# The table of comparisons between a token's logits, moved from SBUF into the free part of the gates' PSUM bank

## The chip, the cores and the metric

The kernel runs on one core of a Trainium2 chip. The metric is the device time of one execution in microseconds (us); the figure given for a kernel is the median of its runs. All data are 32-bit floats.

## The reference

A decoder block over 16 sequences of 256 tokens, 512 wide: a state-space layer, a gated long convolution against a context, and a feed-forward layer with a base product and eight low-rank experts. The experts are where the change lies. Each token takes the two experts with the largest logits:

```python
def _L0_ffn_ref(x, W, b, lora_A, lora_B, gate_w, gate_b):
    K = 2
    ...
    base = x_flat @ W.T + b
    logits = x_flat @ gate_w.T + gate_b
    topk_logits, topk_idx = jax.lax.top_k(logits, K)
    gates = jax.nn.softmax(topk_logits, axis=-1)
    xA = jnp.einsum('nd,erd->ner', x_flat, lora_A)
    delta_all = jnp.einsum('ner,eor->neo', xA, lora_B)
    delta_topk = jnp.take_along_axis(delta_all, topk_idx[:, :, None], axis=1)
    lora_update = jnp.sum(delta_topk * gates[:, :, None], axis=1)
    out = base + SCALING * lora_update
...
x = _layernorm(x + _L0_attn_ref(x, ...), axis=-1)
x = _layernorm(x + _L0_xattn_ref(x, L0_xattn_k, fside_S2_0, ctx_2048, ctx_2048, 8), axis=-1)
x = _layernorm(x + _L0_ffn_ref(x, ...), axis=-1)
```

## The kernel before

The first stage (up to about 760 us) computes the state-space layer for eight groups of 512 tokens and stores the normalised result in `first`. The second stage does the convolution and the feed-forward layer. It is a loop over 32 heads `h` (`HX`), each of 8 positions of all 16 sequences, so 128 tokens. One pass of the loop works on several heads at once: the convolution of head `h`, the feed-forward of head `h - 1`, the low-rank product and the last normalisation of head `h - 2`, and the preparation of head `h + 1`. The order of the instructions on each engine is written out by hand (`manual_schedule`): an engine runs its own instructions in the order of the program, and semaphores connect the engines.

The convolution of a head has two halves, `q` = 0 and 1. In each half TensorE fills four PSUM banks, `y[0]` (blocks 1 and 0) and `y[1]` (blocks 2 and 3):

- `seeded` (L1012) multiplies the pair sums `xs` into the bank of block 3, in `y[1]`; ScalarE copies that to the bank of block 2 (L1019).
- `convolve` adds the full blocks (L1030) and the 64x64 quadrants of the diagonal (L1045).
- `multiplied` (L1080, VectorE) multiplies a pair of banks by the context, `y[1]` first; `reduced` (L1090) sums over eight neighbours. The pool `ps_y` has one buffer of each bank, so the next half's seed follows L1080's reading of `y[1]`.

VectorE also makes the products for the next head (`products`, L157: 128x1024, from a transposed tile in PSUM and the context in SBUF), the reduction `ws` (L942) and the start of the last normalisation (`x3`, L1151, in `finish`). POOL (GpSimd) makes `xs` (L996), differences of Toeplitz blocks `Td` (L1001), the skip products `sk` (L932), the output with residual `ol` (L1259), the folds of its squares (L1185) and the small powers.

The feed-forward of a head: `products_with_gates` puts the logits, the low-rank products `xA`, the mean and the mean square of 128 tokens into one PSUM tile `gl` (pool `ps_t`, two buffers of one bank, tag "tr"): columns 0 to 7 are the logits, 8 to 135 `xA` (`NG` = 136), 136 the mean, 137 the mean square. ScalarE squares the mean (`m2`, L1201), VectorE makes the variance (L1207), POOL the reciprocal root `rs`. Then `gates` turns logits into scaled low-rank products:

- L1118 and L1120: the logits `lg` and their negated maximum; L1122 on ScalarE the exponentials `ex`.
- L1127, L1128: for each of the 64 pairs of experts whether the other logit is equal, and whether it is greater, into the table `cmp` (8 x 2 x 8 words a token). L1129 keeps the equal ones of lower index, with the constant `tri`. L1131 sums the table to a rank.
- L1133: exponentials of the ranks under 1.5, with their sum `den`; L1136 its reciprocal; L1138 the scaled products `xa`, which read `gl` a last time.

In the next pass TensorE transposes `xa` (L1216) and adds the low-rank product (L1222). In the loop this comes just after the base products L1226 and just ahead of the seed L1012 of half 0; on VectorE, L1138 stands directly ahead of the two L1080 of half 1. The last head has no pass to follow: its end is written out after the loop, with `gl` in pool `ps_b` (L1341) and a call of `gates` at L1402. So `gates` is called 32 times.

Of the kernel before, what the change touches and what calls it, by code (L numbers as in the profile page):

```python
# [8 lines left out]
F32 = mybir.dt.float32  # L9
AF = mybir.ActivationFunctionType  # L10
ALU = mybir.AluOpType
# [3 lines left out]
P = 128  # L15
# [9 lines left out]
LN_EPS = 1e-05  # L25
# [6 lines left out]
NE, R = 8, 16  # L32
# [22 lines left out]
NG = NE + ER  # L55
# [3 lines left out]
def layer_norm_stats(nc, pool, nhalf, src, tag):  # L59

    st = pool.tile([P, 6], F32, tag=f"st_{tag}", name=f"st_{tag}")
    nc.vector.bn_stats(st, src)
    mv = pool.tile([P, 2], F32, tag=f"mv_{tag}", name=f"mv_{tag}")
    nc.vector.bn_aggr(mv, st)
    ve = pool.tile([P, 1], F32, tag=f"ve_{tag}", name=f"ve_{tag}")
    nc.vector.tensor_scalar_add(ve, mv[:, 1:2], LN_EPS)  # L66
    rs = pool.tile([P, 1], F32, tag=f"rs_{tag}", name=f"rs_{tag}")
    nc.gpsimd.tensor_tensor(rs, ve, nhalf[:, 0:1], ALU.pow)  # L68
    return mv, rs
# [3 lines left out]
def decoder_kernel(  # L73
# [43 lines left out]
    ps_t = ctx.enter_context(tc.tile_pool(name="ps_t", bufs=2, space=PSUM))  # L117
# [51 lines left out]
    def wait_for(ins, other):  # L169
        tc.add_manual_dep(  # L170
            ins.ins,
            other.ins.name,
            mybir.DependencyInfo(
                mybir.DependencyClass.Sync, mybir.DependencyReason.DATA
            ),
            reason="order",
        )
# [4 lines left out]
    with ExitStack() as s1:  # L182
# [3 lines left out]
        p2 = s1.enter_context(tc.tile_pool(name="p2", bufs=2))  # L186
# [366 lines left out]
        for g in range(groups):  # L553
# [97 lines left out]
            for i, (kind, p) in enumerate(order):  # L651
# [18 lines left out]
                if i == 9:  # L670
# [3 lines left out]
                    for ht in range(HT):  # L674
                        for b in range(GB):
# [4 lines left out]
                                start=(ht == 0),  # L680
                                stop=(ht == HT - 1),
# [67 lines left out]
            def gated(cc, pss):  # L749
# [10 lines left out]
            own = {  # L760
                (r, h): [zs[HC * h + c][:, r * S : (r + 1) * S] for c in range(HC)]
                for r in range(2)
                for h in range(2)
            }
# [99 lines left out]
            else:  # L864
                finish_sums()
                gated(1, spread_heads(1))
                for n, t in enumerate((0, 2, 1, 3)):
# [3 lines left out]
                    for c in range(NI):  # L871
                        for j in range(2):
# [4 lines left out]
                                start=(c == 0 and j == 0),  # L877
                                stop=(c == NI - 1),
                                skip_group_check=True,
# [13 lines left out]
            if g == 0:  # L893
                skip_bc = wp.tile([P, S], F32, name="skip_bc")
                nc.sync.dma_start(skip_bc, skip.partition_broadcast(P))
                w_gl = wp.tile([P, KD, NG + 1], F32, name="w_gl")
# [13 lines left out]
                share = wp.tile([P, P], F32, name="share")  # L910
# [5 lines left out]
    with ExitStack() as s2:  # L916
        w2 = s2.enter_context(tc.tile_pool(name="w2", bufs=1, reuse_waits="tile"))
        p2 = s2.enter_context(tc.tile_pool(name="r2", bufs=2, reuse_waits="tile"))
        ps_b = s2.enter_context(
            tc.tile_pool(name="ps_b", bufs=1, space=PSUM, reuse_waits="tile")  # L920
        )
# [189 lines left out]
            nc.gpsimd.tensor_tensor(rs, var, nhalf[:, 0:1], ALU.pow)  # L1111
            return nm, rs

        def gates(gl, rs):


            lg = p2.tile([P, NE], F32, tag="lg", name="lg")
            nc.vector.scalar_tensor_tensor(lg, gl[:, 0:NE], rs, gb_bc, ALU.mult, ALU.add)  # L1118
            nm = p2.tile([P, 1], F32, tag="nm", name="nm")
            nc.vector.tensor_reduce(nm, lg, AX.X, ALU.max, negate=True)  # L1120
            ex = p2.tile([P, NE], F32, tag="ex", name="ex")
            nc.scalar.activation(ex, lg, AF.Exp, bias=nm)  # L1122
            sq = [P, NE, NE]
            own = lg.unsqueeze(2).to_broadcast(sq)
            other = lg.unsqueeze(1).to_broadcast(sq)
            cmp = p2.tile([P, NE, 2, NE], F32, tag="cmp", name="cmp")
            nc.vector.tensor_tensor(cmp[:, :, 1, :], other, own, ALU.is_equal)  # L1127
            nc.vector.tensor_tensor(cmp[:, :, 0, :], other, own, ALU.is_gt)  # L1128
            nc.vector.tensor_tensor(cmp[:, :, 1, :], cmp[:, :, 1, :], tri, ALU.mult)  # L1129
            rank = p2.tile([P, NE], F32, tag="rank", name="rank")  # L1130
            nc.vector.tensor_reduce(rank, cmp, AX.XY, ALU.add)  # L1131
            den = p2.tile([P, 1], F32, tag="den", name="den")
            nc.vector.scalar_tensor_tensor(  # L1133
                ex, rank, 1.5, ex, ALU.is_lt, ALU.mult, accum_out=den
            )
            nc.vector.reciprocal(den, den)  # L1136
            xa = p2.tile([P, NE, R], F32, tag="xa", name="xa")
            nc.vector.scalar_tensor_tensor(  # L1138
                xa,
                gl[:, NE:NG].rearrange("p (e r) -> p e r", r=R),  # L1140
                den,
                ex.unsqueeze(2).to_broadcast([P, NE, R]),
                ALU.mult,
                ALU.mult,
            )
            return xa
# [12 lines left out]
        def store(h, x3, nb, rs):  # L1159
            res = p2.tile([P, D], F32, tag="res", name="res")  # L1160
            nc.scalar.activation(res, x3, AF.Identity, bias=nb, scale=rs)
            nc.sync.dma_start(out[h * P : (h + 1) * P, :], res)
# [15 lines left out]
        def squares(o_l):  # L1178

            sq = p2.tile([P, D], F32, tag="sq", name="sq")  # L1180
            nc.scalar.activation(sq, o_l.rearrange("p k t -> p (k t)"), AF.Square)

            def folded():
                for n in (D // 2, D // 4):
                    nc.gpsimd.tensor_tensor(sq[:, 0:n], sq[:, 0:n], sq[:, n : 2 * n], ALU.add)  # L1185

            return sq[:, 0:P], folded

        def products_with_gates(o_l, sq):

            gl = ps_t.tile([P, NG + 2], F32, tag="tr", name="gl")
            for kc in range(KD):
                nc.tensor.matmul(  # L1193
                    gl[:, 0 : NG + 1], o_l[:, kc, :], w_gl[:, kc, :],
                    start=(kc == 0), stop=(kc == KD - 1),
                )
            last = nc.tensor.matmul(
                gl[:, NG + 1 :], sq, share[:, 0:1], start=True, stop=True, skip_group_check=True
            )
            m2 = p2.tile([P, 1], F32, tag="m2", name="m2")  # L1200
            wait_for(nc.scalar.activation(m2, gl[:, NG : NG + 1], AF.Square), last)  # L1201
            return gl, m2

        def spread_of(gl, m2):

            var = p2.tile([P, 1], F32, tag="var_b", name="var_b")
            nc.vector.scalar_tensor_tensor(  # L1207
                var, gl[:, NG + 1 :], LN_EPS, m2, ALU.add, ALU.subtract
            )
            rs = p2.tile([P, 1], F32, tag="rs_b", name="rs_b")  # L1210
            nc.gpsimd.tensor_tensor(rs, var, nhalf[:, 0:1], ALU.pow)
            return rs

        def turned_gates(xa, at=None):
            xat = (at or ps_t).tile([ER, P], F32, tag="vp" if at else "tr", name="xat")
            nc.tensor.transpose(xat, xa.rearrange("p e r -> p (e r)"), ident)  # L1216
            xaT = p2.tile([ER, P], F32, tag="xaT", name="xaT")
            nc.scalar.copy(xaT, xat)
            return xaT
# [11 lines left out]
        for h in range(HX):  # L1231
# [8 lines left out]
            if h:  # L1240
# [6 lines left out]
                if rest is not None:  # L1247
                    base, o_r, xa = rest
# [6 lines left out]
            if ff:  # L1255
# [9 lines left out]
                sq, folded = squares(o_l)  # L1265
# [36 lines left out]
            if ff:  # L1302
                gl, m2 = products_with_gates(o_l, sq)
                rs = spread_of(gl, m2)
                base = ps_b.tile([P, D], F32, tag="base", name="base")
                feed_forward(base, o_l, (0,), True)
# [13 lines left out]
                sk_next = skip_sums(h + 1, kv_n)  # L1320
                more_next[2](1)
            if ff:
                xa = gates(gl, rs)
            if nxt:
                convolve(y, kv, T, Td, 1)
                rest = (base, o_l, xa) if ff else None
# [11 lines left out]

        o_f, red_f, y_f, cT_f = last
        tr = ps_t.tile([P, KD, P], F32, tag="tr", name="tr")  # L1340
        gl = ps_b.tile([P, NG], F32, tag="vp", name="gl")  # L1341
        o_l = {}

        def contracted(src, ks):
# [28 lines left out]
        def own(k):  # L1373
            return o_l[k].rearrange("p q t -> p (q t)")

        def norms_and_gates(*ks):
            for k in ks:
                nc.tensor.transpose(tr[:, k, :], own(k), ident)
            for k in ks:
                nc.tensor.matmul(  # L1380
                    gl, own(k), w_gl[:, k, 0:NG], start=(k == 0), stop=(k == 3),
                    skip_group_check=True,
                )

# [9 lines left out]
        contracted(y_f[2].unsqueeze(1), (2,))  # L1394
        contracted(y_f[1][:, 1:2, :], (3,))
        norms_and_gates(0, 1)
        feed(0)
        norms_and_gates(2, 3)
        for k in (1, 2, 3):
            feed(k)  # L1400
        _, rs = layer_norm_stats(nc, p2, nhalf, tr.rearrange("p c l -> p (c l)"), "b")
        xaT = turned_gates(gates(gl, rs))  # L1402
        store(*ready)
        nc.tensor.matmul(base, xaT, w_lb, start=False, stop=True, skip_group_check=True)
        x3 = p2.tile([P, D], F32, tag="x3", name="x3")
        nc.vector.scalar_tensor_tensor(x3, base, rs, b_bc, ALU.mult, ALU.add)
        mv, rs = layer_norm_stats(nc, p2, nhalf, x3, "c")
# [78 lines left out]
```

## Time and profile before

| | |
|---|---|
| median of 3 runs | 1428.67 us (1428.57 to 1429.22) |
| the profiled execution | 1429.05 us, of which the profile's span is 1427.3 |
| mean granted TensorE clock | 0.998 |
| busy over the span: TensorE, VectorE, ScalarE, POOL | 99%, 85%, 29%, 34% |
| busy from 790 to 1390 us: TensorE, VectorE, ScalarE, POOL | 599.7, 553.4, 173.6, 347.4 of 600 us |

The profile is one execution. Each instruction has a start, a duration and, where its engine sat idle before it, the event that ended the idle time. "PE" is a matmul and "PEld" the load of its stationary operand, which may overlap the matmul before it. A tensor operation in this kernel's convolution appears as two PE instructions. The ends of matmuls are modelled, so a busy TensorE isn't TensorE at its full rate. "Issue" is time in which an engine waited for nothing that the profile shows. The busy time of a VectorE instruction includes the time for which it is held up after it has started. Line numbers are those of the kernel before.

### The profile page before, as it was taken

The numbers are of one execution on the slowest core, as the hardware profiler recorded it, in microseconds if no ns is written. First come the engines' busy times: TensorE is split into PE (matmuls) and PEld (weight loads), VectorE is DVE, ScalarE is ACT, GpSimd is POOL, SyncE is SP. The second block draws the span as 40 slices with busy tenths as digits, with TensorE's granted clock in tenths as the row PEclk, the third lists the DMA queues.
The fourth block names the chain that finished last, engine by engine and source line by source line (L and its number), as shares of the span: only waits on it lengthen the run. The fifth ranks groups of instructions, "written<-read, shape, count | busy, mean of one in ns | idle before, by whom it ended". The sixth has DMA issues, their size and how long they took to land.

```text
span 1427.3 us, 18820 instructions
## 1 busy us (share of the span) xinstructions
PE 1413.3 (99%) x6882; PEld 906.7 (64%) x6882; DVE 1211.9 (85%) x2133; ACT 415.2 (29%) x902; POOL 492.4 (34%) x662
## 2 busy tenths in 40 slices
PE   8999999999999999999999999999999999999997
PEld 7788888887888888888884444444444444444443
DVE  6988878788888787887848999999999999999996
ACT  2423323233232332322302222222222232223221
POOL 5450011110100101002005556556555655565562
PEclk9999999999999999999999999999999999999999
DMA  8014111120211201212012221221122122212200
GB/s 300 33 39 131 45 47 45 38 83 8 69 60 38 83 9 39 82 45 84 15 38 85 67 63 55 72 70 57 62 67 74 45 74 67 65 54 74 67 26 23
DMA packets 49164, 89.15 MB, mean 62 GB/s; under 512 B 8880, under 2 KB 13360, under 8 KB 49072
## 3 DMA queue, kind: packets, MB, share of 16 engines
q1 hardware_dynamic: 49072, 87.96, 19.3%
q8 instruction: 54, 0.88, 0.3%
q14 instruction: 38, 0.31, 0.1%
HBM read 70.62 MB, written 17.32 MB: 62 GB/s over the span
## 4 chain that ended last, share of the span: by engine, by line
PE 97%; DVE 1%; issue 1%; DMA 0%; SPq 0%; POOL 0%; POOLq 0%; ACT 0%; DVEq 0%
PE mm L330 21%; PE y L1030 15%; PE s L330 14%; PE y L1045 12%; PE base L1226 8%; PE s L782 6%; PE mm L782 6%; PE y L1012 4%; PE gl L1193 2%; PE base L1222 2%; PE tr L147 1%; PE xm L599 1%; PE mm L739 1%; PE mm L873 1%; PE s L873 1%
## 5 line engine op out<-in xcount | busy, mean ns | idle before, releaser
L1080 DVE TENSOR_TENSOR pr<-y,cT 128x1024 f32<-128x1024 f32 x126 | 148.1, 1217 | 45.4 <-PE y L1045 45.4
L1045 PE MATMUL y<-kv 64*64 64x512 f32 x1536 | 179.6, 598 | 0.0
L588 DVE SCALAR_TENSOR_TENSOR acc<-xi,wc,acc 128x512 f32<-128x512 f32 x192 | 142.3, 755 | 7.4 <-ACT acc L584 1.7
L1090 DVE TENSOR_REDUCE red<-pr 128x128 f32<-128x1024 f32 x126 | 147.1, 1208 | 0.0
L157 DVE TENSOR_TENSOR kv<-tr,cT 128x1024 f32<-128x1024 f32 x124 | 145.4, 1213 | 0.0
L1030 PE MATMUL y<-kv 128*128 128x512 f32 x272 | 128.0, 594 | 1.8 <-DVE pr L1080 1.7
L1045 PEld LDWEIGHTS y<-kv 64*64 64x64 f32 x1536 | 52.2, 132 | 119.0 <-issue 96.7
L1226 PE MATMUL base<-w_f,ol 128*128 128x512 f32 x248 | 124.0, 603 | 0.0
L1030 PE MATMUL y<-kv,Td 128*128 128x512 f32 x248 | 116.5, 592 | 0.0
L68 POOL TENSOR_TENSOR rs_a<-ve_a,nhalf 128x1 f32<-128x1 f32 x32 | 19.0, 594 | 243.0 <-DVE ve_a L66 243.0
L1259 POOL TENSOR_TENSOR ol<-o,red 128x512 f32<-128x512 f32 x31 | 39.4, 1270 | 179.9 <-DVE red L1090 179.9
L391 POOL TENSOR_TENSOR rstd<-ms,nhalf 128x4 f32<-128x4 f32 (+1 forms) x9 | 8.5, 950 | 251.0 <-DVE ms L389 251.0
L1030 PEld LDWEIGHTS y<-kv 128*128 128x128 f32 x272 | 50.9, 189 | 67.8 <-issue 34.1
L330 PE MATMUL mm<-XT,w_z 128*128 128x256 f32 x384 | 90.7, 379 | 0.0
L1030 PEld LDWEIGHTS y<-kv,Td 128*128 128x128 f32 x248 | 47.1, 190 | 59.3 <-issue 59.3
L1019 ACT COPY y<-y 64x512 f32<-64x512 f32 x120 | 67.0, 558 | 56.3 <-PE y L1012 54.3
L996 POOL TENSOR_TENSOR xs<-kv 128x512 f32<-128x512 f32 x63 | 80.4, 1277 | 0.1
L330 PEld LDWEIGHTS mm<-XT,w_z 128*128 128x128 f32 x384 | 73.0, 190 | 9.9
L330 PE MATMUL mm<-xnT,w_z 128*128 128x256 f32 x288 | 70.8, 382 | 0.0
L1012 PE MATMUL y<-xs,kv 128*128 128x512 f32 x120 | 63.5, 611 | 0.7 <-issue 0.7
L1226 PEld LDWEIGHTS base<-w_f,ol 128*128 128x128 f32 x248 | 42.4, 191 | 30.9 <-issue 30.9
L330 PE MATMUL s<-XT,w_xi 128*128 128x256 f32 x256 | 61.0, 380 | 0.5 <-DVE XT L226 0.3
(283 smaller groups left out, 2814.7 us busy)
## 6 DMA issues: line engine op xcount, KB each, us to landing
cT<-in_ctxT SPq DMA_DIRECT2D x32, 384.0 KB
kv<-in_toep SPq DMA_DIRECT2D x32, 384.0 KB
xt<-in_x SPq DMA_DIRECT2D x32, 256.0 KB
spread<-both SPq DMA_DIRECT2D x32, 256.0 KB
first<-xt SPq DMA_DIRECT2D x32, 256.0 KB
vn<-first SPq DMA_DIRECT2D x32, 256.0 KB
out<-res SPq DMA_DIRECT2D x31, 256.0 KB
xnT<-in_xT SPq DMA_DIRECT2D x7, 1024.0 KB
```

The costliest lines, as they stand in the source:

```text
L157: last = nc.vector.tensor_tensor(kv[:, q, k * BQ : (k + NL // 2) * BQ], vT[:, q, blks].rearrange("p k (b i) -> p (k b) i", i=NH).unsqueeze ...
L330: nc.tensor.matmul(ps, w[:, p, a, kc, :], Xs[b][:, kc, :], start=start and kc == 0, stop=stop and kc == 1, skip_group_check=upon,)
L588: ins = nc.vector.scalar_tensor_tensor(acc, xi[:, :, k : k + S], wc[:, c, k : k + 1], acc, ALU.mult, ALU.add)
L782: nc.tensor.matmul(ps, own[a][c][:, n * P : (n + 1) * P], w_o[b][c], start=start and c == 0, stop=stop and c == HC - 1, skip_group_check=upon,
L996: return nc.gpsimd.tensor_tensor(xs[:, q], moving(kv, q, 0), moving(kv, q, 1), ALU.add)
L1012: nc.tensor.matmul(seed, T[:, SHARED_AT, :], xs[:, q], start=True, stop=True)
L1019: nc.scalar.copy(bank_of(y, 2)[b : b + HP], seed[a : a + HP])
L1030: nc.tensor.matmul(bank_of(y, lb), w, moving(kv, q, mb), start=not late and lb not in begun, stop=False, skip_group_check=True,)
L1045: return nc.tensor.matmul(bank_of(y, lb)[cols], T[rows, DIAGONAL_AT, (b - a) * HP : (b - a + 1) * HP], moving(kv, q, lb)[rows], start=star ...
L1080: nc.vector.tensor_tensor(pr.rearrange("p (k b j) i -> p k b j i", k=2, j=NH), y[i].rearrange("p k (b j i) -> p k b j i", j=NH, i=NH), cT[ ...
L1090: nc.vector.tensor_reduce(red[:, q, 2 * i : 2 * i + 2, :].rearrange("p k t -> p (k t)"), pr, AX.X, ALU.add)
L1226: nc.tensor.matmul(base, o_l[:, kc, :], w_f[:, kc, :], start=(first and kc == kcs[0]), stop=False)
```

## The change

The tile `cmp` in SBUF goes. Both tiles `gl` become wider by 2 x 8 x 8 = 128 words, and `gates` is handed these words and lays its table out in them. The bank's other columns keep their places; the matmul and the reading of the mean square name their one column instead of all from there on, and the last head's matmul names columns 0 to 135. Every instruction, its engine and its place in the order stay.

```diff
-        def gates(gl, rs):
+        def gates(gl, rs, room):
...
-            cmp = p2.tile([P, NE, 2, NE], F32, tag="cmp", name="cmp")
+            cmp = room.rearrange("p (a two b) -> p a two b", two=2, b=NE)
             nc.vector.tensor_tensor(cmp[:, :, 1, :], other, own, ALU.is_equal)
             nc.vector.tensor_tensor(cmp[:, :, 0, :], other, own, ALU.is_gt)
             nc.vector.tensor_tensor(cmp[:, :, 1, :], cmp[:, :, 1, :], tri, ALU.mult)
...
-            gl = ps_t.tile([P, NG + 2], F32, tag="tr", name="gl")
+            gl = ps_t.tile([P, NG + 2 + 2 * NE * NE], F32, tag="tr", name="gl")
...
-                gl[:, NG + 1 :], sq, share[:, 0:1], start=True, stop=True, skip_group_check=True
+                gl[:, NG + 1 : NG + 2], sq, share[:, 0:1],
+                start=True, stop=True, skip_group_check=True,
...
-                var, gl[:, NG + 1 :], LN_EPS, m2, ALU.add, ALU.subtract
+                var, gl[:, NG + 1 : NG + 2], LN_EPS, m2, ALU.add, ALU.subtract
...
-                xa = gates(gl, rs)
+                xa = gates(gl, rs, gl[:, NG + 2 :])
...
-        gl = ps_b.tile([P, NG], F32, tag="vp", name="gl")
+        gl = ps_b.tile([P, NG + 2 * NE * NE], F32, tag="vp", name="gl")
...
-                    gl, own(k), w_gl[:, k, 0:NG], start=(k == 0), stop=(k == 3),
+                    gl[:, 0:NG], own(k), w_gl[:, k, 0:NG], start=(k == 0), stop=(k == 3),
...
-        xaT = turned_gates(gates(gl, rs))
+        xaT = turned_gates(gates(gl, rs, gl[:, NG:]))
```

## The prediction

> **What bounds the kernel now.** I read the page first, then the chain that ended last in order of time, then the timeline around one call of `gates`. The page's fourth part says who sets the end:
>
> ```profile
> PE 97%; DVE 1%; issue 1%; DMA 0%; SPq 0%; POOL 0%; POOLq 0%; ACT 0%; DVEq 0%
> ```
>
> Taken alone this says that VectorE (DVE) work is free. Whether a matmul on that chain ran at its own pace has to be read from its pieces. The chain of one head in order of time (start, us, what):
>
> ```profile
> 1017.51 1.72 PE base L1226 x4
> 1019.23 0.11 PE xat L1216
> 1019.33 1.08 PE y L1012 x2
> 1020.41 0.86 PE base L1222 x2
> ...
> 1029.66 0.86 PE y L1012 x2
> ```
>
> Each tensor operation here is two instructions of 0.43 us. The seed matmul at line 1012 takes 0.86 us in one half of the head, but 1.08 where it follows the transpose of the gates (`xat`). So 0.22 us is lost in the second place. The transpose itself isn't the reason: near the end, at 1407.73, the same transpose is followed by four L1030 instructions in 1.72 us, which is 4 x 0.43 with nothing lost.
>
> The timeline shows what the seed waits for (DVE and POOL lines, then the weight load PEld; start, us):
>
> ```profile
> 1014.03 0.21 DVE L1127 TENSOR_TENSOR cmp<-lg 128x64 f32<-128x64 f32 x1
> 1014.10 1.49 POOL L932 TENSOR_TENSOR sk<-kv,skip_bc 128x512 f32<-128x512 f32 x1
> 1014.16 1.50 DVE L1128 TENSOR_TENSOR cmp<-lg 128x64 f32<-128x64 f32 x1
> 1015.53 1.28 POOL L996 TENSOR_TENSOR xs<-kv 128x512 f32<-128x512 f32 x1
> 1015.59 1.30 DVE L1129 TENSOR_TENSOR cmp<-cmp,tri 128x64 f32<-128x64 f32 x1
> ...
> 1017.33 0.17 DVE L1133 SCALAR_TENSOR_TENSOR ex<-rank,ex 128x8 f32<-128x8 f32 x1
> ...
> 1018.00 2.34 DVE L1080 TENSOR_TENSOR pr<-y,cT 128x1024 f32<-128x1024 f32 x2
> ...
> 1019.29 0.30 PEld L1012 LDWEIGHTS y<-xs,kv 128*128 128x128 f32 x2 [0.51 <-issue]
> ```
>
> The seed writes bank 3, in `y[1]`, which DVE reads with the first of the two L1080. That one ends at 1018.00 + 1.215 = 1019.21, and the weight load starts 0.08 later. The profile puts the pause down to "issue", but two other heads settle it: where L1080 starts at 1142.11 its end is 1143.32 and the load starts at 1143.39; from 1389.70 it is 1390.92 and 1390.99. The load follows it by 0.07 each time. In these two heads the chain shows 0.28 and 0.38 us of issue ahead of the seed as well. So TensorE is the engine of the chain, and DVE's queue holds it back once a head.
>
> On DVE two 128x64 operations cost 1.5 and 1.3 us. The trace's answers for single lines (ns min/median/max):
>
> ```profile
> L1127 DVE TENSOR_TENSOR cmp<-lg x32: 212/216/481, 787.0 to 1417.2; 128x64 f32<-128x64 f32 x32
> L1128 DVE TENSOR_TENSOR cmp<-lg x32: 215/1510/1527, 787.2 to 1417.4; 128x64 f32<-128x64 f32 x32
> L1129 DVE TENSOR_TENSOR cmp<-cmp,tri x32: 217/1303/1310, 788.6 to 1417.5; 128x64 f32<-128x64 f32 x32
> L1080 DVE TENSOR_TENSOR pr<-y,cT x126: 1211/1215/1226, 761.8 to 1400.3; 128x1024 f32<-128x1024 f32 x126
> L1151 DVE SCALAR_TENSOR_TENSOR x<-base,rs_b,b_bc x31: 737/740/748, 795.5 to 1410.6; 128x512 f32<-128x512 f32 x31
> ```
>
> Alone (the last two calls, with no POOL work beside them) all three take 0.21 to 0.22. In the other 30 heads L1128 ends as POOL's `sk` ends and L1129 as `xs` ends, 0.07 and 0.08 later. L1080 and L1151 have one input in PSUM and one in SBUF, run beside POOL's operations too (L1151 at 1022.52 beside `ol` from 1022.74), and never stretch.
>
> **What the Trainium skill says.** "SBUF — State Buffer", section "Who interferes with whom": a DVE instruction with two SBUF inputs contends with a GpSimd instruction that reads SBUF, whichever is second blocks until the other ends, and one with at most one SBUF input doesn't contend outside the two-port modes. The rows above agree: 1.3 to 1.5 us against a steady 1.215. "Perfetto Trace Analysis", section "Optimizing Scalar/DVE Operations": an access costs DVE about 60 ns in SBUF and 125 in PSUM. This trace shows no such difference for a PSUM input (L1080 1215 ns; L157 reads 1214 from PSUM and 1219 from SBUF); it has no DVE instruction that writes PSUM. "PSUM — Partial Sum Buffer", section "PSUM bank collisions raise a hardware error": two engines may not touch one bank's same partitions at once. Of this bank's other users the last, ACT's `m`, ends at 1028.90, and L1127 comes at 1034.66, so order costs nothing.
>
> **The change part by part.** It adds and removes no instruction, transfer or buffer: `gl` grows to 266 words, below the 512 of the other tiles of its tag. Four DVE instructions a call, 32 calls, change an operand's place.
>
> L1127 and L1128 still read `lg` twice from SBUF and write to PSUM. I keep them as they are: L1127 slips in between `Td` and `sk`, L1128 ends behind `sk` at 1015.66.
>
> L1129 now reads `cmp` from PSUM and `tri` from SBUF, the form of L1080. It should no longer wait for `xs`: 0.22 us instead of 1.30. In the call without POOL, L1133 starts 0.56 after the end of L1128 (1405.28 to 1405.84). Here that is 1015.66 + 0.56 = 1016.22 instead of 1017.33, or 1.11 earlier.
>
> **What is late next.** L1133 reads `rank` and `ex`, both in SBUF, and `xs` runs until 1016.81. By the same rule it blocks. Its form does so in this trace: an L588 at 22.89 beside POOL took 1.10 against a median of 0.75. It then ends at about 1016.89 as L1129 does now, against 1017.50: 0.61 earlier. I take 0.61; 1.11 is the other end.
>
> Price of PSUM as destination and for the reduction L1131: from 0 (the nearest rows, PSUM inputs) to 4 x 65 = 260 ns a call, my estimate from the skill's 125 - 60; a faster write than to SBUF can't be excluded, -50. I take 100 where nothing covers it. In the 30 heads the first 1016.81 - 1016.22 = 0.59 is covered by L1133's wait for `xs`; without that wait, 1.11 - 0.26 = 0.85 still remains.
>
> What the path gains: L1080 ends 0.61 earlier, at 1018.60, and the seed's load could start at 1018.67. TensorE wants it at the start of `xat`, 1019.06. It is ready 0.39 early and the pause goes. Over the 30 heads the pieces above 0.86 add up to 6.87 us, the issue ahead of them to 0.67: 7.54 in all. In the head at 1390 the pause is 0.24 + 0.38 = 0.62, just what DVE gives back; up to 0.05 may stay. The rest of DVE's 0.61 becomes idle time: before the other L1080 of a head it waits 1.35 us for L1045 now, and will wait about 1.35 + 0.61 - 0.23 = 1.7. `y[1]` can't be taken earlier than L1045 ends, 1016.92, which I have kept. POOL's `ol` and the folds start earlier, ahead of matmuls that don't wait for them.
>
> The last call (1417.2 to 1418.9) lies on the path with no POOL beside it: plus 0.1.
>
> Sum, against the profiled execution: 1429.05 - 7.54 + 0.05 + 0.1 = 1421.7. That execution is 0.38 above the median of 1428.67, so 1421.3 on the scale of the median.
>
> **The rivals.**
>
> *The gap is missed (slower).* L1127 starts 0.07 us ahead of `sk`. If, at its place between `Td` and `sk`, the PSUM destination makes it more than about 0.1 late, `sk` goes first: L1127 takes the 1.5 us, L1128 the 1.3, and L1129 comes after `xs` on top. L1131 then starts 0.16 behind L1128's end (as in the free call) where it now starts 0.04 behind L1129's, and two PSUM accesses add 0.13: 0.25 x 30 = 7.5 us, 1436. For it: the narrow margin. Against: at 1137.85 L1127 waited through `Td` (0.48 us) and still came ahead of `sk`. 6 in 100.
>
> *L1129 blocks all the same*, because the destination or `tri` takes the shared port. DVE loses 2 x 0.065 a head behind `xs`, 3.9 us, and 0.3 at the end, or nothing if PSUM is as cheap: 1428.7 to 1432.9. Against: L1080 and L1151. 4 in 100, half within 0.2%.
>
> *The pause is TensorE's own*, so that DVE only idles more: 1428.8. Against: the two heads where the load moved with L1080. 2 in 100.
>
> *Part of the gain*: L1128 or POOL shifts and 0.1 to 0.2 of each pause stays, 1423 to 1427. 6 in 100, most of it still over 0.2%.
>
> **How the numbers follow.** The main case has 82 in 100: 1420.3 (pause gone, a PSUM write slightly cheap, 0.5 us between chips) to 1422.2. The range goes on to 1424.0 to take in the larger part of the partial gains. About 0.2%, 2.9 us, is what a measurement of this kernel can tell from no change. Faster: 0.82 + 0.05 of the partial cases = 0.87. Within: 0.01 + 0.02 + 0.02 = 0.05. Slower: 0.06 + 0.02 = 0.08.
>
> **What would show it.** L1129 with a median near 220 ns, L1133 stretched to 0.5 or 0.6, L1012 at 0.86 in both halves, DVE idle before L1080 near 1.7 a head, a head of 20.4 us instead of 20.63. It is wrong if L1129 stays at 1.3, if L1127 is the one that stretches, or if L1012 keeps 1.08 though L1080 comes earlier.

## The result, and the profile after

The changed kernel takes 1421.83 us (median of 5 runs, 1421.24 to 1422.03) against 1428.67 (5 runs, 1428.46 to 1429.22): a ratio of 0.9951, with an interval of 0.9936 to 0.9965. A second series, run later, gave 1422.16 against 1428.82, a ratio of 0.9952 (0.9940 to 0.9965). The forecast was 1421.3, in a range of 1420.3 to 1424.0.

The profiled execution took 1421.88 us with a span of 1420.1, so 7.2 us of span are gone. (From line 1198 on, line numbers are one higher than before.) The page's chain still belongs to TensorE:

```profile
PE 97%; DVE 1%; issue 1%; DMA 1%; SPq 0%; POOL 0%; POOLq 0%; ACT 0%; DVEq 0%
```

That line doesn't tell whether the change has worked: a kernel below that gains nothing (only that source left in SBUF) has the same 97%. The chain of one head in order of time (start, us, what) shows the difference:

```profile
1014.44 0.59 PE tr L147 x4
1015.02 1.72 PE base L1227 x4
1016.74 0.11 PE xat L1217
1016.85 0.86 PE y L1012 x2
...
1026.96 0.86 PE y L1012 x2
```

The seed L1012 takes 0.86 us in both halves. It takes 0.86 in every one of the 30 heads that had a pause, and no issue time stands ahead of it. From seed to seed a head is 20.41 us (1016.85 to 1037.26) where it was 20.63.

The same stretch on VectorE and POOL, from the timeline:

```profile
1011.55 0.22 DVE L1127 TENSOR_TENSOR gl<-lg 128x64 f32<-128x64 f32 x1
1011.61 1.48 POOL L932 TENSOR_TENSOR sk<-kv,skip_bc 128x512 f32<-128x512 f32 x1
...
1011.81 1.38 DVE L1128 TENSOR_TENSOR gl<-lg 128x64 f32<-128x64 f32 x1
1013.06 1.26 POOL L996 TENSOR_TENSOR xs<-kv 128x512 f32<-128x512 f32 x1
1013.22 0.23 DVE L1129 TENSOR_TENSOR gl<-gl,tri 128x64 f32<-128x64 f32 x1
1013.49 0.29 DVE L1131 TENSOR_REDUCE rank<-gl 128x8 f32<-128x128 f32 x1
1013.89 0.46 DVE L1133 SCALAR_TENSOR_TENSOR ex<-rank,ex 128x8 f32<-128x8 f32 x1
...
1014.86 2.35 DVE L1080 TENSOR_TENSOR pr<-y,cT 128x1024 f32<-128x1024 f32 x2
...
1016.58 0.30 PEld L1012 LDWEIGHTS y<-xs,kv 128*128 128x128 f32 x2 [0.29 <-issue]
```

L1129 runs beside `xs` and takes 0.23 us. L1133, with its two inputs in SBUF, starts while `xs` still runs and is held until 0.03 us after its end (1013.06 + 1.26 = 1014.32; 1013.89 + 0.46 = 1014.35). L1080 lets `y[1]` go at 1014.86 + 1.214 = 1016.07. With the 0.07 to a weight load the seed could be loaded at 1016.15; TensorE loads it at 1016.58. So 0.43 us of slack is there now. Over all 32 calls (ns min/median/max):

```profile
L1127 DVE TENSOR_TENSOR gl<-lg x32: 221/222/480, 787.1 to 1409.8; 128x64 f32<-128x64 f32 x32
L1128 DVE TENSOR_TENSOR gl<-lg x32: 232/1387/1422, 787.3 to 1410.0; 128x64 f32<-128x64 f32 x32
L1129 DVE TENSOR_TENSOR gl<-gl,tri x32: 231/232/233, 788.8 to 1410.3; 128x64 f32<-128x64 f32 x32
...
L1133 DVE SCALAR_TENSOR_TENSOR ex<-rank,ex x32: 168/459/467, 789.4 to 1410.9; 128x8 f32<-128x8 f32 x32
```

What VectorE has won beyond the pause is idle time ahead of the other L1080. The waits from 780 to 1390 us (total us, times, longest), before and after:

```profile
DVE pr L1080 <- PE y L1045: 40.6, 30, 1.4
```

```profile
DVE pr L1080 <- PE y L1045: 52.9, 30, 1.8
```

That is 1.35 and 1.76 us a head.

### The profile page after: what moved, and what is told of

It is laid out like the page before. It is cut to its first block, busy times and chain, and to the rows that moved or that the text cites. A ratio compares the mean times of both kernels' runs of the same rounds, so it can differ in the third digit from the quotient of the medians.

```text
span 1420.1 us, 18821 instructions
## 1 busy us (share of the span) xinstructions
PE 1405.9 (99%) x6882; PEld 906.5 (64%) x6882; DVE 1191.5 (84%) x2133; ACT 415.0 (29%) x902; POOL 492.1 (35%) x662
## 4 chain that ended last, share of the span: by engine, by line
PE 97%; DVE 1%; issue 1%; DMA 1%; SPq 0%; POOL 0%; POOLq 0%; ACT 0%; DVEq 0%
PE mm L330 21%; PE y L1030 15%; PE s L330 14%; PE y L1045 12%; PE base L1227 8%; PE s L782 6%; PE mm L782 6%; PE y L1012 4%; PE gl L1193 2%; PE base L1223 2%; PE tr L147 1%; PE xm L599 1%; PE mm L739 1%; PE mm L873 1%; PE s L873 1%
## 5 line engine op out<-in xcount | busy, mean ns | idle before, releaser
L1080 DVE TENSOR_TENSOR pr<-y,cT 128x1024 f32<-128x1024 f32 x126 | 148.1, 1217 | 57.8 <-PE y L1045 57.8
L1045 PE MATMUL y<-kv 64*64 64x512 f32 x1536 | 179.6, 598 | 0.0
L1045 PEld LDWEIGHTS y<-kv 64*64 64x64 f32 x1536 | 52.2, 132 | 119.0 <-issue 96.6
L996 POOL TENSOR_TENSOR xs<-kv 128x512 f32<-128x512 f32 x63 | 80.2, 1272 | 0.1
L1012 PE MATMUL y<-xs,kv 128*128 128x512 f32 x120 | 61.3, 593 | 0.0
```

The source lines that it names most:

```text
L996: return nc.gpsimd.tensor_tensor(xs[:, q], moving(kv, q, 0), moving(kv, q, 1), ALU.add)
L1012: nc.tensor.matmul(seed, T[:, SHARED_AT, :], xs[:, q], start=True, stop=True)
L1045: return nc.tensor.matmul(bank_of(y, lb)[cols], T[rows, DIAGONAL_AT, (b - a) * HP : (b - a + 1) * HP], moving(kv, q, lb)[rows], start=star ...
L1080: nc.vector.tensor_tensor(pr.rearrange("p (k b j) i -> p k b j i", k=2, j=NH), y[i].rearrange("p k (b j i) -> p k b j i", j=NH, i=NH), cT[ ...
```

## The experiments

The theory: of the five operand places that moved (the results of L1127, L1128 and L1129, the sources of L1129 and L1131), only the source of L1129 matters. With one input in SBUF in place of two it doesn't wait for POOL; L1080 comes earlier, and the gain ends where TensorE's own pace begins. The rivals: that the place of the results or PSUM as such helps; that VectorE's queue is still the bound, so that each further saving would count; that VectorE has so much idle time that nothing on it counts.

**Only the source of L1129 in PSUM.** The table is back in SBUF; L1127 alone writes to the bank.

```diff
+            cmp = p2.tile([P, NE, 2, NE], F32, tag="cmp", name="cmp")
+            eq = room.rearrange("p (a two b) -> p a two b", two=2, b=NE)[:, :, 1, :]
+            nc.vector.tensor_tensor(eq, other, own, ALU.is_equal)
...
+            nc.vector.tensor_tensor(cmp[:, :, 1, :], eq, tri, ALU.mult)
```

> The changed kernel, but the table is back in SBUF; only the 64 results of L1127 are in PSUM, so L1129 reads PSUM and the constant and writes SBUF as before. Theory (only L1129's second SBUF input made it wait for POOL): L1129 near 0.22 us, L1133 stretched to about 0.45, the seed L1012 at 0.86 in both halves, 1421.5 to 1421.8 (the last call, on the path, a little shorter than the 0.27 us that the full table in PSUM costs there). Rival (the place of the table matters: writes to SBUF share the port with POOL): L1129 stays at 1.3 and the time at 1428.7.

1420.95 us (1420.83 to 1420.99) against 1428.88, a ratio of 0.9945 (0.9932 to 0.9958). The multiplication and the weighting of the exponentials, by line of that kernel:

```profile
L1130 DVE TENSOR_TENSOR cmp<-gl,tri x32: 210/211/219, 788.0 to 1409.4; 128x64 f32<-128x64 f32 x32
...
L1134 DVE SCALAR_TENSOR_TENSOR ex<-rank,ex x32: 168/602/617, 788.7 to 1410.1; 128x8 f32<-128x8 f32 x32
```

64 words in place of 128 have the whole effect. (They are L1127's result as well, but L1127 alone takes 0.21 to 0.22 us in either place.) The time is 0.55 us below the range that I had given. The last call costs nothing here: the long piece of issue at the end of the chain, in which it lies, is 5.94 us in place of 6.22. In the profiled execution the rest of the difference lies ahead of the second stage, whose first seed starts at 761.87 in place of 762.49, though the code of the first stage is the same. What the multiplication no longer waits for, the next instruction with two SBUF inputs waits for: 602 ns here, 459 in the changed kernel, where it comes later.

**All but that source in PSUM.**

```diff
+            eq = p2.tile(sq, F32, tag="eq", name="eq")
+            nc.vector.tensor_tensor(eq, other, own, ALU.is_equal)
             nc.vector.tensor_tensor(cmp[:, :, 0, :], other, own, ALU.is_gt)
+            nc.vector.tensor_tensor(cmp[:, :, 1, :], eq, tri, ALU.mult)
```

> The changed kernel, but the results of L1127 are in SBUF: the table is in PSUM, L1129 reads two SBUF inputs and writes PSUM. Theory: L1129 at 1.3 us again, the pause of 0.22 ahead of the seed is back, PSUM writes and the reduction add a few hundredths behind the wait: 1428.7 to 1430. Rival (the destination matters): L1129 at 0.23 and 1421.8.

1429.28 us (1428.74 to 1429.74), a ratio of 1.0003 (0.9995 to 1.0012): the gain is gone.

```profile
L1130 DVE TENSOR_TENSOR gl<-eq,tri x32: 232/1194/1199, 788.1 to 1417.4; 128x64 f32<-128x64 f32 x32
```

With two inputs in SBUF the multiplication waits again though it writes PSUM, and the seed is at 1.10 us (1018.79). The place of the results doesn't matter for this wait.

**The kernel before, with POOL's second pair sum later.** No operand moves; the L996 that L1129 waited for is put behind L1133.

```diff
                 sk_next = skip_sums(h + 1, kv_n)
-                more_next[2](1)
             if ff:
                 xa = gates(gl, rs)
+            if nxt:
+                pair = more_next[2](1)
+                if ff:
+                    wait_for(pair, weighed[-1])
```

> The kernel before, with the table in SBUF; only POOL's second pair sum (L996, half 1 of the next head) is put behind L1133, so that it doesn't run beside L1129. Theory (the wait for POOL is all that the change took away): L1128 keeps 1.5 us, L1129 falls to 0.22, L1133 to 0.17, L1080 about 1.1 us earlier than before, the pause gone: 1421.0 to 1421.5, some 0.3 below the changed kernel since the last call keeps its SBUF speed. Rival (PSUM itself is what helps): 1428.7 or slower.

1421.14 us (1420.69 to 1422.23), a ratio of 0.9948 (0.9935 to 0.9961). In the timeline the multiplication (L1131 of this kernel) has both inputs in SBUF and isn't held, since POOL's sum comes after it:

```profile
1011.25 1.50 DVE L1130 TENSOR_TENSOR cmp<-lg 128x64 f32<-128x64 f32 x1
1012.67 0.21 DVE L1131 TENSOR_TENSOR cmp<-cmp,tri 128x64 f32<-128x64 f32 x1
...
1013.31 0.17 DVE L1135 SCALAR_TENSOR_TENSOR ex<-rank,ex 128x8 f32<-128x8 f32 x1
...
1013.57 1.28 POOL L996 TENSOR_TENSOR xs<-kv 128x512 f32<-128x512 f32 x1 [0.91 <-DVE ex L1135]
```

The same gain without PSUM: what the change took away is the wait for POOL.

**Both.** The changed kernel with the same move of the pair sum.

> The changed kernel and the pair sum behind L1133: VectorE is earlier by another 0.3 us a head, since L1133 doesn't block any more. Theory (TensorE at its own pace is the bound after the change): the time stays at 1421.8 within 0.3, the idle time ahead of L1080 grows from 1.76 to about 2.05 us a head. Rival (VectorE's queue is still the bound): 30 x 0.3, so about 9 us less, 1413.

1421.39 us (1421.07 to 1421.54), a ratio of 0.9949 (0.9935 to 0.9963). The idle time ahead of L1080 is 61.0 us over 30 heads, 2.03 a head against 1.76, and the time is what it was. What VectorE saves after the change isn't worth anything here: TensorE's own pace is the bound.

**Time put back, ahead of L1138.** A reduction over a constant, one input in SBUF, in three sizes.

```diff
+            idle = p2.tile([P, 1], F32, tag="idle", name="idle")
+            nc.vector.tensor_reduce(idle, b_bc[:, 0:128], AX.X, ALU.max)
             xa = p2.tile([P, NE, R], F32, tag="xa", name="xa")
```

> The changed kernel with a reduction of 128 words of a constant ahead of L1138 in every call: some 0.2 us more on VectorE that contends with nothing. The seed's weight load in a steady head wants its bank 0.43 us after L1080 has let it go. Theory: covered in 29 heads, late by 0.15 in the last, and 0.2 on the path at the end: 1422.0 to 1422.4. Rival (VectorE has no slack): 30 x 0.2 = 6 us, 1428.

1421.68 us (1421.21 to 1421.80): nothing lost, but the dose (the time by which L1080 comes later) was smaller than meant. L1136 to L1080 is 0.52 us (1014.03 to 1014.55), in the changed kernel 0.47 (1014.39 to 1014.86). The reduction fell into the time in which L1138 waits for L1136's result, and added 0.05.

> The same with 512 words, some 0.61 us. Theory: 0.43 covered, 0.18 late in each of 29 heads, 0.57 in the last, 0.6 at the end: 1421.8 + 5.2 + 0.6 + 0.6 = 1428.2 (1427 to 1430). Rival (VectorE has over 0.6 us of slack, since its idle time is 1.76 a head): 1422.4. Rival (no slack): 1440.

1424.37 us (1423.35 to 1424.50), below the range that I had given. L1136 to L1080 is 0.92 us, so the dose was 0.45 and not 0.61, just over the slack of 0.43:

```profile
1014.41 0.16 DVE L1136 RECIPROCAL den<-den 128x1 f32<-128x1 f32 x1
1014.49 0.67 DVE L1138 TENSOR_REDUCE idle<-b_bc 128x1 f32<-128x512 f32 x1
1015.07 0.34 DVE L1140 SCALAR_TENSOR_TENSOR xa<-gl,den,ex 128x128 f32<-128x128 f32 x1
1015.33 2.35 DVE L1080 TENSOR_TENSOR pr<-y,cT 128x1024 f32<-128x1024 f32 x2
...
1016.61 0.30 PEld L1012 LDWEIGHTS y<-xs,kv 128*128 128x128 f32 x2 [0.31 <-issue]
```

The seeds' pieces exceed 0.86 by 1.35 us in all, with 0.26 of issue: 1.6 us in the loop. The end has more than its dose: the long piece of issue there is 7.61 us in place of 6.22. Of these 1.39 us 0.46 are the dose and 0.93 the last head's low-rank product on TensorE, two matmuls that take 2.06 us in place of 1.13. The profile has a granted TensorE clock of 0.54 over that product (1414.1 to 1416.3), where the changed kernel has 1.00 (1412.4 to 1413.7). Together that is 3.0 us, and from the second stage's first seed to the end of the span this execution is 2.9 us longer than the changed kernel's. The price was off, the slack was right; one more size tests that.

> As the kernel with 512 words ahead of L1138, with a second reduction of 256 words behind it: 0.34 us more at the pace of reductions here (1.13 us for 1024, 0.2 for 128). Theory: the first one moved L1080 by 0.47, just over the slack of 0.43 us, so all of the second shows, at 0.34 us a call: 31 calls, 1424.4 + 10.6 = 1435.0 (1433.5 to 1436.5). Rival (the small loss of the first was something else, and slack is left): under 1428.

1438.38 us (1437.76 to 1438.80), above the range that I had given. L1136 to L1080 is 1.37 us, a dose of 0.90: the second reduction added 0.45 too, and not 0.34. Of that, 0.90 - 0.43 = 0.47 shows in 29 heads, all of it in the last head and at the end: 13.6 + 1.8 = 15.4, or 1437.2. The loop of the chain has 15.2 us of pauses, and the end is 2.00 us longer: 0.9 the dose, and 1.1 the last transpose and product at a granted clock that falls to 0.50 (0.44 and 2.08 us in place of 0.30 and 1.13). The clock is the larger part of what the sum left out. In both kernels TensorE stands idle longer ahead of that transpose than in the changed one (1.67 and 2.11 us against 1.20); why the clock fell wasn't tried. So doses of 0.05, 0.45 and 0.90 us a call cost 0, 2.5 and 16.5 us in all, and about 1 us of each of the last two is the lower clock at the end. The pauses in the loop, 0, 1.6 and 15.2 us, bend at the slack that the profile shows.

**The same reduction of 128 words, ahead of L1127.**

> The changed kernel with the reduction of 128 words ahead of L1127 instead, so that L1127 comes some 0.15 us after POOL's sk has begun. Theory (turns are taken at the gaps between POOL's operations): L1127 stretches to 1.3 or more, L1128 to 1.3, L1129 0.23 after them, L1080 about 0.95 us later, the seed late by 0.5 in each of 30 heads: 1436 to 1440. Rival (0.2 us is covered as at the other place): 1422.0 to 1422.4.

1437.33 us (1436.53 to 1437.52), a ratio of 1.0058 (1.0044 to 1.0072).

```profile
1016.97 0.28 DVE L1127 TENSOR_REDUCE idle<-b_bc 128x1 f32<-128x128 f32 x1
1017.04 1.48 POOL L932 TENSOR_TENSOR sk<-kv,skip_bc 128x512 f32<-128x512 f32 x1
...
1017.16 1.45 DVE L1129 TENSOR_TENSOR gl<-lg 128x64 f32<-128x64 f32 x1
1018.49 1.27 POOL L996 TENSOR_TENSOR xs<-kv 128x512 f32<-128x512 f32 x1
1018.65 1.20 DVE L1130 TENSOR_TENSOR gl<-lg 128x64 f32<-128x64 f32 x1
1019.88 0.23 DVE L1131 TENSOR_TENSOR gl<-gl,tri 128x64 f32<-128x64 f32 x1
```

The first comparison (L1129 here) misses the gap ahead of `sk` (the moment between two POOL instructions) and waits for it, the second waits for `xs`, and the multiplication comes on top. A delay of about 0.2 us became a loss of 15.5. This is the rival that the prediction put on the slower side, brought about by a delay: its mechanism is real, and in the changed kernel only its condition, a late L1127, wasn't met.

**The last call in SBUF.**

```diff
-        xaT = turned_gates(gates(gl, rs, gl[:, NG:]))
+        xaT = turned_gates(gates(gl, rs, None))
```

> The changed kernel, but the last call, the one with no POOL beside it and nothing to cover it, has its table in SBUF. Theory: 0.27 us less, 1421.5. Rival (PSUM costs nothing there): 1421.8.

1421.38 us (1421.15 to 1421.48), a ratio of 0.9947 (0.9934 to 0.9959). That is 0.45 below the first series of the changed kernel and 0.78 below the second, and these two differ by 0.33 themselves. So I read it from the chain in order of time: the long piece of issue at the end, in which the last call lies, is 5.94 us in place of 6.22, or 0.28.

**The fewest words in PSUM.** In the loop only L1127's results, in the last call none.

> The fewest words in PSUM: in the loop only the results of L1127 (the table in SBUF), in the last call none. Theory: the pause is gone and the last call costs nothing: the shortest version, 0.25 to 0.3 below the changed kernel run beside it. Rival: no different from it within 0.1.

1421.16 us (1420.83 to 1421.51), a ratio of 0.9947 (0.9933 to 0.9960).

> The changed kernel once more, beside the other two on one chip: 1421.2 to 1422.0.

1422.16 us (1421.71 to 1422.26), on the same chip, 0.16 above the range that I had given. The version with the fewest words is 1.0 us shorter, more than the 0.28 expected. Of this, 0.28 is the last call (5.94 and 6.22 again). In the profiled executions the spans differ by 0.6, of which the second stage's first seed explains 0.36: it starts at 761.97 and 762.33, though the first stage is the same code. From that seed to the end of the span the profiled executions fall into two groups: 657.57 us for the changed kernel, its repetition and the one with both moves, and 657.30 for this version, the first, the third and the one with the last call in SBUF. So 0.27 us, the last call, is all that sets these four below the changed kernel in the second stage; why the first stage, with the same code, varies between executions stays open.

## Why the prediction was right

*What bounds.* The reading of the chain held. The 0.22 us that the seed took too long was a wait for VectorE, although the profile named "issue": the seed follows L1080 when time is added (1.10 us with 0.24 of issue ahead of it at the largest dose), and it falls back to 0.86 in all three ways of taking the wait away.

*What is removed.* L1129 from 1.30 to 0.23 us, forecast 0.22, for the reason given: the first three experiments leave the source of L1129, and POOL beside it, as the only condition.

*What is late next.* L1133 stretched to 459 ns, forecast 0.5 to 0.6, and ends with `xs`; it came 0.70 us after the end of L1128 and not 0.56, so it had less to wait. From the end of L1045 to L1080 the time fell from 1.08 (1016.92 to 1018.00) to 0.42 us (1014.44 to 1014.86): 0.66 gained, 0.61 forecast. Idle time ahead of the other L1080 1.76, forecast 1.7; slack ahead of the seed 0.43, forecast 0.39.

*The size.* All 7.54 us of pauses went, the last head's included. The last call cost 0.27 us (L1127 to L1131: 0.52 before, 0.79 after), where I took 0.1, with the spacing of L1127 and L1128 unchanged, in bounds of -0.05 to 0.26. That is just outside the bounds, and not in the way that they assume, by longer accesses: the starts moved apart (below). The span gives 7.54 - 0.27 = 7.27, measured 7.2. The other term that was off is the step from the profiled execution to the median: I took off the 0.38 us by which the execution before lay above its median, and the one after lies only 0.05 above. Which execution is profiled is chance. Together these make the 0.5 us between 1421.3 and 1421.83.

*The rivals.* The missed gap didn't come about: L1127 stayed 0.06 us ahead of `sk`. That L1129 would block all the same, that the pause was TensorE's own, and that a part would stay, are all out.

## What to carry to other kernels

When one engine carries 97% of the chain, look for the same instruction with two durations in it: here 1.08 and 0.86 us, and the difference was a wait for another engine that the share hides. The gain ends where that wait ends: VectorE became 0.66 us a head faster, and 0.22 of it counted. The small VectorE instructions here that lasted until the POOL instruction beside them ended (1303 ns, against 217 alone) were waiting for it, and all had two inputs in SBUF. Moving one of the two inputs of L1129, or the POOL instruction, was enough; the next instruction with two such inputs was the next to wait. Before time is added ahead of a chain of such turns, see which gap it makes the chain miss.

## What was not expected

The price of PSUM wasn't in the durations. The three instructions that write it grew by 9 to 17 ns (alone: 212 to 221, 215 to 232, 217 to 231), the reduction that reads it by 5. But their starts moved apart. The last call before and after:

```profile
1417.23 0.21 DVE L1127 TENSOR_TENSOR cmp<-lg 128x64 f32<-128x64 f32 x1
1417.37 0.21 DVE L1128 TENSOR_TENSOR cmp<-lg 128x64 f32<-128x64 f32 x1
1417.50 0.22 DVE L1129 TENSOR_TENSOR cmp<-cmp,tri 128x64 f32<-128x64 f32 x1
1417.75 0.29 DVE L1131 TENSOR_REDUCE rank<-cmp 128x8 f32<-128x128 f32 x1
```

```profile
1409.76 0.22 DVE L1127 TENSOR_TENSOR gl<-lg 128x64 f32<-128x64 f32 x1
1410.01 0.23 DVE L1128 TENSOR_TENSOR gl<-lg 128x64 f32<-128x64 f32 x1
1410.28 0.23 DVE L1129 TENSOR_TENSOR gl<-gl,tri 128x64 f32<-128x64 f32 x1
1410.55 0.29 DVE L1131 TENSOR_REDUCE rank<-gl 128x8 f32<-128x128 f32 x1
```

From start to start 0.14, 0.13 and 0.25 us became 0.25, 0.27 and 0.27. The two comparisons write different columns of one bank, and in the built program the second now waits for the first's semaphore, and the multiplication for the second's; before, the second waited for nothing. That is the distance of a dependent pair, as L1129 and L1131 have in both kernels. Where only the first comparison writes the bank the starts are 0.13 and 0.14 apart again (1409.13, 1409.26, 1409.40). So the cost goes with the waits that the program has for one bank. Whether the chip would need this distance without them wasn't tried.

The turns that VectorE and POOL take are fine. In the changed kernel L1127 starts 0.06 us ahead of `sk` and takes 0.22 us; with the delay ahead of it the same comparison starts 0.12 us behind `sk` and takes 1.45.
